# Self attention of an encoder-decoder layer: score groups side by side, eight PSUM banks in one round, value products summed in SBUF

## The chip, the cores and the metric

The kernel runs on one core of a Trainium2 chip. The metric is the device time of one execution in microseconds (us); the time before is the median of three runs, 2924.71 us (2924.21 to 2924.82). A core has five engines with a queue of instructions each: PE (matrix products into PSUM), DVE (vector), ACT (scalar), POOL (GpSimd) and SP, which here issues the DMAs. PSUM has eight banks of 128 x 512 float32; DVE and ACT read it, POOL doesn't. An engine runs its queue in order and waits on semaphores for the others.

## The reference

One encoder layer over a context of 77 rows and one decoder layer over 2048 rows, for two batch elements, all in float32; the width is 512, with 16 heads of 32. The part that the change touches is the decoder's causal self attention with a relative bias:

```python
def _mha(xq, xkv, w_in, b_in, w_out, b_out, bias):
    ...
    q = (xq @ wq.T + bq).reshape(Bq, Tq, H, hd).transpose(0, 2, 1, 3)
    k = (xkv @ wk.T + bk).reshape(Bq, Tk, H, hd).transpose(0, 2, 1, 3)
    v = (xkv @ wv.T + bv).reshape(Bq, Tk, H, hd).transpose(0, 2, 1, 3)
    scores = jnp.einsum('bhqd,bhkd->bhqk', q, k) / jnp.sqrt(jnp.asarray(hd, xq.dtype))
    scores = scores + bias[None]
    attn = jax.nn.softmax(scores, axis=-1)
    out = jnp.einsum('bhqk,bhkd->bhqd', attn, v)
    out = out.transpose(0, 2, 1, 3).reshape(Bq, Tq, D)
    return out @ w_out.T + b_out
...
causal = jnp.where(jnp.arange(Tt)[None, :] > jnp.arange(Tt)[:, None], -jnp.inf, 0.0)
sb = _rel_bias(dec_rel_self, Tt, Tt) + causal[None]
yn = _ln(y, dec_n1_s, dec_n1_b)
y = y + _mha(yn, yn, dec_sa_in_w, dec_sa_in_b, dec_sa_out_w, dec_sa_out_b, sb)
```

After it come cross attention to the encoder's 77 rows and a feed-forward layer.

## The kernel before

**Units, pieces and pairs.** Self attention runs first, up to about 1776 us of the span, and the feed-forward layer with the cross attention after it. It is cut into 128 *units* in the order b, m, g, t: batch element (2), block of 512 query rows (m, 4), group of four heads (g, 4), tile of 128 query rows in the block (t, 4). A unit has i + 1 blocks of 128 keys, with i = 4 m + t. `pieces(i)` cuts these into pieces of at most four blocks (4, 4, 4, 3 for fifteen; 4, 4, 3, 2 for thirteen), and the loop at the end takes two consecutive pieces of a unit as a *pair*. With m = 0 and 1 a unit has one pair, with m = 2 and 3 two; there are 192 pairs.

**What is done for a piece.** `scores` takes four banks, one per head, and writes one 128 x (up to 512) product into each (L361): a *score group*. The four heads stand in four quarters of PE's rows, so the four products run beside each other. DVE then empties bank after bank into `pp`, with the row maximum (L370); the last two blocks of a unit get bias and mask on the way (L377), and the unit's maximum is put together (L384). The exponentials are ACT's, one per head over the unit's whole row (L387). For m of 1 and over they are held back in `late_exps`, and `exps(k)` issues k of them at a chosen place.

**The turn.** `turn(pair)` transposes the probabilities on PE (L411), four 128 x 128 tiles into one bank: a *load*. For m of 1 and over a load holds the four heads of one key block, so a full pair has eight. Each load is copied to `pts`, by ACT (L417) or by DVE (L415); before, the first half of the loads is ACT's and the second half DVE's, and an exponential is issued after the fourth load and one at the end. A load needs the exponentials of all four heads.

**The values.** `values` multiplies the turned probabilities with `vv` (L428), 32 rows of output per head, and sums over all key blocks of the unit in bank 7, where the four tiles of a group of heads stand beside each other. At the group's end the bank is copied whole to `oT` (L434). A unit later `divide` multiplies it by the reciprocals of the sums (L447 on PE, L448 on DVE), and some units later `out_job` uses it.

**The banks.** `bank()` hands out banks in turn. Seven go round, and the eighth is the values'. A matmul that gets a bank waits until the engine that reads its last contents has done so, and PE's queue waits with it.

**The order.** Everything is issued in the order in which the loop calls it, each engine in its own queue. Scoring is two units ahead: a unit's pieces are scored when the unit two before has been turned as far (`may_score`). Between two units stands `slot(n + 1)`: the projections (`q_job`, `k_job`, `v_job`, `out_job`: four matmuls of 512 columns, one bank each), the norms of the next block, the encoder's stages (in the first 27 units) and a first cross attention (in units 65 to 92). So in the long rows the order on PE is: turn, scores, values, scores; turn, slot, scores, values, scores; and so on. The loop's body, before:

```python
            turn(pair)
            ...
            if ends and n + 1 < end:
                slot(n + 1)
            if may_score():
                score_next()
            exps(2 if units[n][1] == 1 else 1)
            for p in pair:
                values(*p)
            while may_score() and (len(pair) > 1 or units[n][1] == 0):
                score_next()
```

The numbers of units count from 0: unit 54 is b = 0, m = 3, g = 1, t = 2 and has fifteen key blocks.

Of the kernel before, what the change touches and what calls it, by code (L numbers as in the profile page):

```python
# [10 lines left out]
F32 = mybir.dt.float32  # L11
AF = mybir.ActivationFunctionType
ALU = mybir.AluOpType
# [4 lines left out]
P = 128  # L18
B, T, S, D = 2, 2048, 77, 512
H, HD, DFF = 16, 32, 2048  # L20
NC = D // P
NF = DFF // P
HC = P // HD
MB = 512
NMB = T // MB
TB = MB // P
# [28 lines left out]
def tile_encoder_decoder(ctx: ExitStack, tc: tile.TileContext, ins, out):  # L55
    nc = tc.nc
# [92 lines left out]
    with (  # L149
# [7 lines left out]
        vv = ac.tile([P, T // P, D], F32, name="vv")  # L157
# [6 lines left out]
        oT_all = ac.tile([P, 6, TB * P], F32, name="oT")  # L164
        bv = ac.tile([P, D], F32, name="row_sa_bv")
        bo = ac.tile([P, D], F32, name="row_dec_sa_out_b")
        psum = ps.tile([P, 8, 512], F32, name="psum")
        count = {"bank": 0, "banks": 7, "pts": 0, "oT": 0, "mm": 0}

        def bank():  # L170

            i = count["bank"] % count["banks"]
            count["bank"] += 1
            return psum[:, i, :]

        def in_turn(what, tile):
            i = count[what] % tile.shape[1]
            count[what] += 1
            return tile[:, i, :]

        def rows4(r):
            return slice(r * HD, (r + 1) * HD)


        nTs, qTs, ots, sums_of = {}, {}, {}, {}
# [132 lines left out]
        units = [(b, m, g, t) for b in range(B) for m in range(NMB) for g in range(NC) for t in range(TB)]  # L318
# [20 lines left out]
        def exps(k):  # L339

            for _ in range(min(k, len(late_exps))):
                late_exps.pop(0)[1]()
# [52 lines left out]
        got = {}  # L395

        def turn(pieces):

            first = units[pieces[0][0]][1] == 0
            loads = []  # L400
            for n, k0, kn in pieces:
                ks = range(k0, k0 + kn)
                if first:
                    loads += [[(n, k, r) for k in ks] for r in range(HC)]
                else:
                    loads += [[(n, k, r) for r in range(HC)] for k in ks]
            for o, load in enumerate(loads):
                pt = bank()
                pts = in_turn("pts", pts_all).rearrange("p (x q) -> p x q", q=P)
                for x, (n, k, r) in enumerate(load):  # L410
                    nc.tensor.transpose(pt[:, ts(x, P)], state[n]["p"][r][:, ts(k, P)], ident)  # L411
                    got[n, k, r] = pts[:, x, :]
                w = len(load) * P
                if o % 2 if first else o >= (len(loads) + 1) // 2:
                    nc.vector.tensor_copy(pts[:, : len(load), :], pt[:, :w])  # L415
                else:
                    nc.scalar.copy(pts[:, : len(load), :], pt[:, :w])  # L417
                if o == min(3, len(loads) - 1):
                    exps(1)
            exps(1)  # L420

        def values(n, k0, kn):
            b, m, g, t = units[n]
            i = m * TB + t
            for k in range(k0, k0 + kn):
                ot = psum[:, 7, :].rearrange("p (t q) -> p t q", q=P)
                for r in range(HC):
                    nc.tensor.matmul(  # L428
                        ot[rows4(r), t, :], vv[:, k, ts(g * HC + r, HD)], got.pop((n, k, r)),
                        start=(k == 0), stop=(k == i),  # L430
                    )
                if t == TB - 1 and k == i:
                    o = ots[b, m, g] = in_turn("oT", oT_all)
                    (nc.vector.tensor_copy if m else nc.scalar.copy)(o, psum[:, 7, :])  # L434

        def divide(b, m, g):

# [455 lines left out]
        for x, (b, m) in enumerate(blocks):  # L893
            u = x * NU
            first = m == 0
# [77 lines left out]
        def slot(n):  # L973
            for f in light[n]:
                f()
            for _, run, _ in jobs[n]:
                load_next()
                run(loaded[ran[0]])
                ran[0] += 1
            if n == 5:  # L980
                load_next()
# [35 lines left out]
        def w_1_load(i):  # L1017

            nc.sync.dma_start(w_1[:, :, ts(i, D)], wchunk("dec_ff1_wT", i * D))
# [220 lines left out]
        def may_score():  # L1240

            if at[0] == len(stream):
                return False
            n, k0, kn = stream[at[0]]
            same = n >= 2 and units[n][:2] == units[n - 2][:2]
            return n < 2 or turned_to[n - 2] >= (min(k0 + kn, size[n - 2]) if same else size[n - 2])

        def score_next():
            n, k0, kn = stream[at[0]]
            scores(n, k0, kn)  # L1250
            scored_to[n] = k0 + kn
            at[0] += 1
# [4 lines left out]
        i = 0  # L1257
        while i < len(stream):
            n = stream[i][0]
            pair = [p for p in stream[i : i + 2] if p[0] == n]  # L1260
            while scored_to.get(n) != size[n]:
                score_next()
            while any(u == n for u, _ in late_exps):
                exps(1)
            ends = pair[-1][1] + pair[-1][2] == size[n]
            if ends:
                for f in ahead[n + 1]:
                    f()
            turn(pair)
            if n == end - 2:  # L1270
                for _, k0, _ in pair:
                    w_1_load(k0 // 4)
            turned_to[n] = pair[-1][1] + pair[-1][2]
            if ends and n + 1 < end:
                slot(n + 1)
            if may_score():
                score_next()
            exps(2 if units[n][1] == 1 else 1)
            for p in pair:
                values(*p)  # L1280
            while may_score() and (len(pair) > 1 or units[n][1] == 0):
                score_next()
            i += len(pair)

        xt_ring += [sb.tile([P, D], F32, name="xt", tag="xt", bufs=2) for _ in range(2)]
# [71 lines left out]
```

## Time and profile before

| | |
|---|---|
| median of three runs | 2924.71 us |
| the profiled execution | 2926.65 us, of which its span 2924.9 us |
| granted PE clock, mean | 0.99 |
| self attention, m = 2 of b = 0 (407 to 640 us) | PE 231.9, DVE 196.7, ACT 135.7, POOL 7.1 us busy of 233 |
| self attention, m = 3 of b = 0 (640 to 929 us) | PE 285.4, DVE 246.9, ACT 177.9, POOL 7.2 us busy of 289 |
| score products, L361 | 353.2 us on PE |
| turns, L411 | 546.2 us on PE |
| value products, L428 | 278.9 us on PE |

How to read it: the page gives each engine's busy time, and PE's is modelled, since its matmuls overlap: a matmul that waits for its bank can count as busy. So the turns are better judged by the time from their first instruction to the first of what follows, and by the lines that name a releaser ("<-DVE mx L377": the wait before it was ended by DVE's instruction at line 377 on tile mx). In the order of time each line is a run of equal instructions: its start, its length, the engine, the line of the code, the operation, the tiles and their shapes, and how many; L361 and L428 show two instructions for a matmul.

### The profile page before, as it was taken

How to read it: one execution, taken by the hardware profiler on the slowest of the kernel's cores; microseconds unless marked ns; L12 is line 12 of the kernel's file. 1: busy time of each engine (PE TensorE's matmuls, PEld its weight loads, DVE VectorE, ACT ScalarE, POOL GpSimd, SP SyncE). 2: the span in 40 equal slices, each digit the busy share in tenths (PEclk: the TensorE clock that was granted, in tenths of full speed). 3: DMA queues.
4: the chain of work that ended last, by engine and by line, in shares of the span. 5: the costliest groups of instructions: out<-in, count | busy, mean ns of one | idle time of the engine just before them, and what ended most of it. 6: DMA issues, size and time to landing. Idle time of an engine off the chain costs nothing.

```text
span 2924.9 us, 60758 instructions
## 1 busy us (share of the span) xinstructions
PE 2867.7 (98%) x24440; PEld 2017.3 (69%) x24440; DVE 2121.4 (73%) x5958; ACT 1303.9 (45%) x2431; POOL 732.7 (25%) x594
## 2 busy tenths in 40 slices
PE   8899999999999999999999999999999999999999
PEld 5457666666666556666666667877777777777788
DVE  4767688888987788788888894757575757575745
ACT  3344456546665446555556673323232323232321
POOL 0100000000000101000000004565556364646464
PEclk9899999999999999999999999999999999999999
DMA  6413301201111502211201116000001000000000
GB/s 173 101 54 112 100 16 52 67 16 45 34 41 56 141 23 73 71 27 54 55 16 38 41 31 206 1 30 1 29 1 38 10 29 1 30 1 30 1 15 15
DMA packets 117644, 137.11 MB, mean 47 GB/s; under 512 B 18240, under 2 KB 73072, under 8 KB 117234
## 3 DMA queue, kind: packets, MB, share of 16 engines
q1 hardware_dynamic: 117362, 133.22, 15.7%
q8 instruction: 192, 3.15, 0.4%
q14 instruction: 90, 0.74, 0.1%
HBM read 111.33 MB, written 21.86 MB: 46 GB/s over the span
## 4 chain that ended last, share of the span: by engine, by line
PE 84%; DVE 13%; ACT 1%; issue 1%; DMA 1%; SPq 0%; POOL 0%; DVEq 0%; ACTq 0%; POOLq 0%
PE psum L1160 13%; PE psum L411 12%; PE psum L1131 11%; PE psum L361 10%; PE psum L428 7%; DVE pp L370 5%; PE psum L230 4%; PE psum L811 4%; PE psum L206 4%; PE psum L751 4%; PE psum L242 4%; PE psum L217 3%; DVE pp L377 3%; PE psum L791 2%; PE psum L765 1%
## 5 line engine op out<-in xcount | busy, mean ns | idle before, releaser
L387 ACT ACTIVATE pp<-pp,nm 128x128 f32<-128x128 f32 (+15 forms) x512 | 614.2, 1210 | 197.9 <-DVE nm L384 195.1
L370 DVE TENSOR_SCALAR_CACHE_REDUCE pp<-psum 128x512 f32<-128x512 f32 (+3 forms) x1024 | 558.0, 589 | 53.7 <-PE psum L361 51.7
L411 PE MATMUL psum<-ident,pp 128*128 128x128 f32 x4352 | 546.2, 278 | 17.7 <-DVE mx L377 11.8
L411 PEld LDWEIGHTS psum<-ident,pp 128*128 128x128 f32 x4352 | 472.7, 142 | 130.5 <-DVE pp L370 56.5
L417 ACT COPY pts<-psum 128x512 f32<-128x512 f32 (+3 forms) x592 | 298.8, 577 | 517.2 <-PE psum L411 391.4
L1114 POOL TENSOR_TENSOR vv<-pp 128x512 f32<-128x512 f32 x320 | 425.6, 1345 | 168.2 <-PE psum L1131 148.0
L361 PE MATMUL psum<-kT,q 32*128 32x512 f32 (+3 forms) x2560 | 353.2, 579 | 7.5 <-DVE mx L377 3.5
L415 DVE COPY pts<-psum 128x512 f32<-128x512 f32 (+2 forms) x544 | 329.8, 659 | 41.0 <-PE psum L411 39.3
L428 PEld LDWEIGHTS psum<-pts,vv 128*32 128x32 f32 x8704 | 226.2, 110 | 123.9 <-issue 116.9
L428 PE MATMUL psum<-pts,vv 128*32 128x128 f32 x8704 | 278.9, 276 | 0.0
L1146 DVE TENSOR_TENSOR kT<-kT,psum 128x512 f32<-128x512 f32 x256 | 166.7, 681 | 114.6 <-PE psum L1131 108.9
L276 POOL TENSOR_TENSOR rstd<-rstd,mhalf 128x1 f32<-128x1 f32 x32 | 18.2, 570 | 920.7 <-DVE rstd L275 860.7
L377 DVE CUSTOM_DVE_ANT_0 pp<-psum,bias 128x256 f32<-128x256 f32 (+1 forms) x512 | 209.6, 409 | 24.2 <-PE psum L361 16.7
L361 PEld LDWEIGHTS psum<-kT,q 32*128 32x128 f32 x2560 | 119.7, 184 | 152.2 <-issue 97.8
L1149 ACT ACTIVATE kT<-kT,vecs 128x256 f32<-128x256 f32 x256 | 115.1, 499 | 194.2 <-DVE kT L1146 194.2
L1160 PE MATMUL psum<-vv 128*128 128x256 f32 x768 | 176.9, 381 | 0.0
L1131 PE MATMUL psum<-oT,vv 128*128 128x256 f32 x736 | 166.5, 380 | 0.0
L1160 PEld LDWEIGHTS psum<-vv 128*128 128x128 f32 x768 | 143.1, 190 | 26.8 <-issue 9.5
L1144 ACT COPY kT<-psum 128x512 f32<-128x512 f32 x124 | 69.7, 589 | 205.9 <-DVE kT L1146 135.5
L1131 PEld LDWEIGHTS psum<-oT,vv 128*128 128x128 f32 x736 | 138.8, 190 | 24.5 <-issue 6.4
L1114 DVE TENSOR_TENSOR vv<-kT 128x512 f32<-128x512 f32 x160 | 136.3, 867 | 12.3 <-PE psum L1160 12.1
L257 POOL TENSOR_TENSOR xr<-xr,row_dec_sa_out_b 128x512 f32<-128x512 f32 x30 | 38.1, 1273 | 372.8 <-DMA xr<-in_x_dram 354.5
(175 smaller groups left out, 3961.9 us busy)
## 6 DMA issues: line engine op xcount, KB each, us to landing
wqk<-in_dec_sa_in_wT_dram SPq DMA_DIRECT2D x64, 256.0 KB, 3.8
bias<-tz SPq DMA_DIRECT2D x128, 128.0 KB, 3.7
wbig<-in_dec_sa_in_wT_dram SPq DMA_DIRECT2D x8, 1024.0 KB, 8.1
vv<-in_enc_ff_wT_dram SPq DMA_DIRECT2D x8, 1024.0 KB, 5.5
wbig<-in_dec_sa_out_wT_dram SPq DMA_DIRECT2D x8, 1024.0 KB, 7.6
vv<-y SPq DMA_DIRECT2D x32, 256.0 KB, 3.4
out_dram<-vv SPq DMA_DIRECT2D x32, 256.0 KB, 2.0
xt<-in_x_dram SPq DMA_DIRECT2D x30, 256.0 KB, 3.7
```

What stands on the lines that cost most here:

```text
L361: nc.tensor.matmul(banks[r][:, : kn * P], q[rows4(r), ts(t, P)], kT[rows4(r), g, k0 * P : (k0 + kn) * P], start=True, stop=True,)
L370: nc.vector.tensor_scalar(p[:, k0 * P : (k0 + far) * P], s[:, : far * P], 1.0, None, ALU.mult, ALU.max, accum_out=st["mx"][:, r, c : c + 1],)
L377: nc.vector.tensor_tensor_reduce(p[:, (i + 1) * P - w : (i + 1) * P], s[:, far * P : kn * P], biases[b, m, g][:, r, 2 * P - w :], 1.0, LOW ...
L387: nc.scalar.activation(p, p, AF.Exp, bias=nm, accum_out=to)
L411: nc.tensor.transpose(pt[:, ts(x, P)], state[n]["p"][r][:, ts(k, P)], ident)
L415: nc.vector.tensor_copy(pts[:, : len(load), :], pt[:, :w])
L417: nc.scalar.copy(pts[:, : len(load), :], pt[:, :w])
L428: nc.tensor.matmul(ot[rows4(r), t, :], vv[:, k, ts(g * HC + r, HD)], got.pop((n, k, r)), start=(k == 0), stop=(k == i),)
L1114: engine.tensor_tensor(dst, quarter(*parts[0], n), quarter(*parts[2], n), SIGN[parts[1]])
L1131: nc.tensor.matmul(mm[:, ts(f, TOK)], a[:, c, ts(f, P)], b[:, c, :], start=(c == 0), stop=(c == 1))
L1146: nc.vector.tensor_tensor(dst, dst, got, SIGN[sign])
L1160: nc.tensor.matmul(mm[:, t, :], lhs[:, c, ts(t, P)], rhs[:, c, :], start=(n == 0 and c == 0), stop=(n == 3 and c == 1),)
```

## The change

The loop now scores as far as it may before the values, and the values of a pair are one call. They get a bank of the round, which now has eight, and are summed there over the pair alone; ACT copies them out, to `oT` for a unit's first pair, and to a tile `more` for a later one, which GpSimd adds to `oT`. Of a turn's loads DVE gets the first three eighths and ACT the rest. The exponential in the middle of a turn is gone, and after the scores three are issued in place of two where m = 1.

```diff
-        count = {"bank": 0, "banks": 7, "pts": 0, "oT": 0, "mm": 0}
+        count = {"bank": 0, "banks": 8, "pts": 0, "oT": 0, "mm": 0}
...
-                if o % 2 if first else o >= (len(loads) + 1) // 2:
+                if o % 2 if first else o < 3 * len(loads) // 8:
                     nc.vector.tensor_copy(pts[:, : len(load), :], pt[:, :w])
                 else:
                     nc.scalar.copy(pts[:, : len(load), :], pt[:, :w])
-                if o == min(3, len(loads) - 1):
-                    exps(1)
             exps(1)
 
-        def values(n, k0, kn):
+        def values(pieces):
+
+            n = pieces[0][0]
             b, m, g, t = units[n]
-            i = m * TB + t
-            for k in range(k0, k0 + kn):
-                ot = psum[:, 7, :].rearrange("p (t q) -> p t q", q=P)
+            ks = [k for _, k0, kn in pieces for k in range(k0, k0 + kn)]
+            ot = bank()[:, :P]
+            for k in ks:
                 for r in range(HC):
                     nc.tensor.matmul(
-                        ot[rows4(r), t, :], vv[:, k, ts(g * HC + r, HD)], got.pop((n, k, r)),
-                        start=(k == 0), stop=(k == i),
+                        ot[rows4(r), :], vv[:, k, ts(g * HC + r, HD)], got.pop((n, k, r)),
+                        start=(k == ks[0]), stop=(k == ks[-1]),
                     )
-                if t == TB - 1 and k == i:
-                    o = ots[b, m, g] = in_turn("oT", oT_all)
-                    (nc.vector.tensor_copy if m else nc.scalar.copy)(o, psum[:, 7, :])
+            if t == 0 and ks[0] == 0:
+                ots[b, m, g] = in_turn("oT", oT_all)
+            dst = ots[b, m, g][:, ts(t, P)]
+            if ks[0] == 0:
+                nc.scalar.copy(dst, ot)
+            else:
+                more = sm.tile([P, P], F32, name="more", tag="more", bufs=1)
+                nc.scalar.copy(more, ot)
+                nc.gpsimd.tensor_tensor(dst, dst, more, ALU.add)
...
             if may_score():
                 score_next()
-            exps(2 if units[n][1] == 1 else 1)
-            for p in pair:
-                values(*p)
             while may_score() and (len(pair) > 1 or units[n][1] == 0):
                 score_next()
+            exps(3 if units[n][1] == 1 else 1)
+            values(pair)
             i += len(pair)
```

## The prediction

> **What bounds the kernel now.** I read the page's busy times first, then its chain, then the groups, then PE and DVE in order of time around one turn of the longest rows.
>
> ```profile
> PE 2867.7 (98%) x24440; PEld 2017.3 (69%) x24440; DVE 2121.4 (73%) x5958; ACT 1303.9 (45%) x2431; POOL 732.7 (25%) x594
> PE 84%; DVE 13%; ACT 1%; issue 1%; DMA 1%; SPq 0%; POOL 0%; DVEq 0%; ACTq 0%; POOLq 0%
> ```
>
> PE sets the end, but 13% of the chain (about 380 us) runs through DVE, by line L370 and L377: DVE emptying score banks. So PE waits for banks at times, although its row shows 98%. The groups say where:
>
> ```profile
> L411 PEld LDWEIGHTS psum<-ident,pp 128*128 128x128 f32 x4352 | 472.7, 142 | 130.5 <-DVE pp L370 56.5
> L417 ACT COPY pts<-psum 128x512 f32<-128x512 f32 (+3 forms) x592 | 298.8, 577 | 517.2 <-PE psum L411 391.4
> L415 DVE COPY pts<-psum 128x512 f32<-128x512 f32 (+2 forms) x544 | 329.8, 659 | 41.0 <-PE psum L411 39.3
> ```
>
> The turns (L411) wait for DVE; ACT idles between its copies, DVE hardly (41.0 us before 544 copies). Now unit 53 to 54 in order of time (start, length, what); PE:
>
> ```profile
> 754.99 1.14 PE L361 MATMUL psum<-kT,q 32*128 32x512 f32 x8
> 756.06 1.52 PE L428 MATMUL psum<-pts,vv 128*32 128x128 f32 x48
> 757.51 1.14 PE L361 MATMUL psum<-kT,q 32*128 32x512 f32 x8
> 758.58 2.46 PE L411 MATMUL psum<-ident,pp 128*128 128x128 f32 x20
> 761.25 0.66 PE L411 MATMUL psum<-ident,pp 128*128 128x128 f32 x4 [0.22 <-DVE mx L377]
> 762.13 1.09 PE L411 MATMUL psum<-ident,pp 128*128 128x128 f32 x8 [0.22 <-DVE mx L377]
> 763.15 1.14 PE L361 MATMUL psum<-kT,q 32*128 32x512 f32 x8
> 764.23 1.96 PE L428 MATMUL psum<-pts,vv 128*32 128x128 f32 x64
> 766.11 1.14 PE L361 MATMUL psum<-kT,q 32*128 32x512 f32 x8
> ```
>
> and DVE:
>
> ```profile
> 756.15 0.69 DVE L370 TENSOR_SCALAR_CACHE_REDUCE pp<-psum 128x512 f32<-128x512 f32 x1 [0.30 <-PE psum L361]
> ...
> 758.67 0.42 DVE L370 TENSOR_SCALAR_CACHE_REDUCE pp<-psum 128x256 f32<-128x256 f32 x1
> ...
> 762.11 0.16 DVE L384 TENSOR_REDUCE nm<-mx 128x1 f32<-128x5 f32 x1
> 762.19 2.48 DVE L415 COPY pts<-psum 128x512 f32<-128x512 f32 x4
> 764.59 0.68 DVE L370 TENSOR_SCALAR_CACHE_REDUCE pp<-psum 128x512 f32<-128x512 f32 x1
> ```
>
> Call the two score groups of a pair A and B, the values V, the eight loads of the turn l0 to l7. With A's start as 0: V 1.07, B 2.52, turn 3.59, next A 8.16. The same turn with no wait takes 3.64 (several in the trace), here 4.57: l5 and l6 wait for DVE. DVE empties A from 1.16 to 3.68 (0.61 a bank), B, a unit's last group with bias and maximum, to 7.28 (0.88 a bank), and only then copies its loads.
>
> **The change, part by part.** All durations from this execution; the sum goes against its 2926.65 us and then moves to the median 2924.71 (1.9 less).
>
> *Scores side by side.* In the trace a group that follows another one starts 0.96 after it, where V or a turn starts 1.07 after. In the built order 135 groups follow a group directly, 21 before: 114 x 0.11 = 12.5 us less on PE at most. It counts only where the turn that follows isn't DVE's.
>
> *What DVE must do before the turn.* B moves ahead of V, but DVE was not idle in between (0.07 from 3.61 to 3.68), so it finishes B at 7.21 in place of 7.28. PE: A 0, B 0.96, V 2.03, turn 3.48, l6 still waits for B's last bank: the turn ends at 8.1 again, not 7.1. Moving B hides nothing here.
>
> *The copies change hands.* Before, ACT copied the first half of a turn's loads, DVE the rest; now DVE the first three of eight, ACT the last five (L415 544 to 392, L417 592 to 744). DVE sheds 152 x 0.62 = 94 us and the 24 copies of oT (16.4 us); that is off the path unless DVE ends a wait. With eight banks round and eight loads, the next A takes the banks of l0 to l3 and B those of l4 to l7 where no slot lies between. Before (seven banks), A took l1 to l4, three of them ACT's, the fourth DVE's first. Now A's first three wait for all of DVE's copies, and those stand behind B's emptying in DVE's queue: 7.13 + 0.69, then 0.62 and 0.62: l2's bank is free at 9.05. So r=2 of the next A starts at 9.1 in place of 8.1, B at 10.06, V at 11.13, the next turn at 13.01. Before that turn started at 767.18, which is 12.19. **Cost +0.8 us**, and behind the waiting matmul all of PE is queued; what is late next is V and the second turn, whose slot then gives DVE time, so it doesn't add up.
>
> The same walk for the other turns that have no slot behind them, with the emptying times of their last group (0.74 a bank for three blocks, 0.53 for two, starts 1.16, 0.95 or 0.73 after a group of 512, 384 or 256):
> - four-block rows (m = 3), t = 1, last group three blocks: DVE done 6.67, l2 free 8.5, +0.90, 4 per batch element; t = 2 (the walk above) +0.84, 3; t = 0 (two blocks behind 512): wait 0.6, less 0.22 and earlier starts, +0.31, 3; t = 3 +0.05, 3; t = 2 of the last g, where V follows the turn, +0.4.
> - m = 2: t = 2 behind a last group of four alone: DVE done 4.75, turn ends 5.64, l2 free 6.6: +0.91, 3, and +0.4 once. t = 1, where three groups now run before V: before A, V, B, C took 5.97 (481.25 to 487.21); V hid 1.88 of DVE's work on A. Now C's banks are A's, so C waits for DVE's 3.06 on A, and V comes after: +0.86, 4. t = 0 and 3: 0. One turn that waits 1.7 (DVE late out of the slot; the slot starts later now, DVE doesn't) gives back 1.2.
> - m = 1: a slot behind every turn; 8 turns, -0.11 or 0: -0.9. Where blocks change: three groups before V +0.5 and +1.1; five groups before V, where V now hides emptying: -1.7.
> - m = 0: one group a unit, order as before: 0.
>
> Per batch element: 0.93 + 3.6 + 2.5 + 0.15 + 0.4 + 2.7 + 0.4 + 3.4 - 1.2 - 0.9 + 0.5 + 1.1 - 1.7 = 12. Two: **+24 us**. Each wait is good to about 0.3 us over some 50 places: +9 to +39.
>
> *V leaves its bank.* 192 copies on ACT, 128x128: the row of L417 in that shape has 268 ns: 51 us, plus 152 x 0.52 = 79 for loads, less 8 x 0.57: ACT +126 us. Cover: in long rows a unit has 10 copies, four exps of 2.0 and two V copies, 13.7 of some 18.6 us. Queued behind the V copy are the next turn's copies, first needed 1.8 us into that turn; l7 reuses V's bank 3.2 us into it. Without the cover, an exp (2.0) ahead of the V copy would hold the turn. The three exps that m = 1 now runs in a row (1.1 each) can end after the turn wants them when the slot keeps ACT busy: 0 to 1.4 us at 8 places, I take 0 since most turns there wait for DVE anyway; range 0 to +11.
>
> *GpSimd adds.* 64 of 128x128. Bounds: 0.55 (128x1, L276) and 1.27 (128x512, L257); by size 0.73: 47 us on an engine that is busy 7 us in the 233 us of m = 2 (407 to 640 us). The sum is read by L448 a unit later, some 15 us: 0. Does it slow DVE? L415's copy has 0.68 both inside and outside GpSimd's 1.27 us adds (13 inside): 0, with 0 to 0.55 x 64 = 35 as the far bound.
> The Trainium skill (GPSIMD Engine Reference, section Specifications) speaks against this part: GpSimd shares its SBUF interface with VectorE and contends with certain VectorE forms, those in a two-port mode or with two SBUF inputs. By that an add could hold DVE for its length, and 64 of them would add up to the 47 us just named; the copies from PSUM in this trace show none of it, so the row decides.
>
> *The eighth bank.* Where slots run several jobs (m = 0 and 1), one more bank may free PE earlier: 0 to -6, since the waits there that name DVE or ACT are few; I take 0.
>
> **Forecast:** 2926.65 + 24 - 1.9 = 2949 us, own range 2930 to 2970.
>
> **The rivals.**
> 1. *Faster: the waits in the turns go and none comes back.* It needs DVE to reach l3 to l6's banks in time, that is, B's emptying to move ahead with B. For it: the row of L411 has 56.5 us behind L370 alone. Against it: DVE has no gap to move into. If so, 30 turns x 0.85 and 12.5: 2887. It decides if DVE idles over 0.9 us between A and B in most pairs.
> 2. *No change:* A's wait is real but a third of what I have (DVE's copies run as soon as their load is there, ahead of the emptying's end). Against it: one queue, in order. 24 - 24 = about 2925.
> 3. *Much slower: ACT.* If the V copy stands behind an exp that waits for DVE's maximum, the turn's copies and the next groups wait 1 us or more in the 64 long pairs: 2949 + 64 = 3013. Against it: the exps ahead of V are of a unit scored a pair earlier, so their maximum is long there.
>
> **How the numbers follow.** Forecast 0.62, rival 1 0.15, rival 2 0.10, rival 3 0.13. Below 0.2% (5.8 us) a measurement can't tell a change here. Faster takes rival 1 and a small share of the rest, 0.17; same 0.11; slower 0.72. The range runs from 2912 to 2980: the forecast's own, all of no change, and the near parts of the rivals.
>
> **What would show it.** In the new trace, behind unit 54's turn, the third matmul of the score group starts about 1 us after the second, released by DVE's copy (L415); turns behind a last group of three or four blocks still take 4.4 to 4.6; V follows B after 1.07; ACT stands idle before most copies of L417; PE's idle time that names ACT stays under 10 us. It is wrong if the score groups behind turns take 0.96 (rival 1 or 2), or if turns wait for ACT (rival 3).

## The result, and the profile after

The changed kernel takes 2973.89 us (median of five runs, 2971.24 to 2975.92) against 2924.71: 1.0165 times as long, 95% interval 1.0153 to 1.0176, or 49 us more. Its profiled execution has a span of 2969.5 us against 2924.9, so 44.6 us of the difference can be looked for in the traces. All of it lies in self attention, whose last value product on PE starts at 1818.3 us in place of 1774.2.

The page after: busy times and the groups of turn and copies (busy, mean ns | idle before, by releaser).

```profile
PE 2881.6 (97%) x24440; PEld 2061.6 (69%) x24440; DVE 2013.0 (68%) x5782; ACT 1421.8 (48%) x2767; POOL 763.4 (26%) x658
...
L411 PE MATMUL psum<-ident,pp 128*128 128x128 f32 x4352 | 544.5, 278 | 44.1 <-ACT pp L387 32.3 <-DVE mx L377 9.9 <-DVE nT L301 0.5
L411 PEld LDWEIGHTS psum<-ident,pp 128*128 128x128 f32 x4352 | 475.9, 142 | 106.5 <-ACT pp L387 39.3 <-issue 29.1 <-DVE mx L377 28.0
L417 ACT COPY pts<-psum 128x512 f32<-128x512 f32 (+2 forms) x744 | 379.4, 586 | 196.9 <-PE psum L411 157.1 <-issue 17.7 <-DVE pp L370 14.7
```

DVE lost 108 us of work and ACT took 118, and yet PE is later. The 56.5 us that the turns waited for DVE's emptying (L370) no longer head the list; a wait that was small before does: PE waits 32.3 us for exponentials (ACT, L387), 2.4 before. The rest of the new time is hidden in PE's "busy" and shows only in the order of time. Unit 54 on PE:

```profile
771.02 2.56 PE L411 MATMUL psum<-ident,pp 128*128 128x128 f32 x20
773.80 0.66 PE L411 MATMUL psum<-ident,pp 128*128 128x128 f32 x4 [0.22 <-DVE mx L377]
774.68 1.09 PE L411 MATMUL psum<-ident,pp 128*128 128x128 f32 x8 [0.22 <-DVE mx L377]
775.70 2.95 PE L361 MATMUL psum<-kT,q 32*128 32x512 f32 x16
778.58 1.95 PE L428 MATMUL psum<-pts,vv 128*32 128x128 f32 x64
```

and on DVE:

```profile
774.65 0.16 DVE L384 TENSOR_REDUCE nm<-mx 128x1 f32<-128x5 f32 x1
774.73 1.88 DVE L415 COPY pts<-psum 128x512 f32<-128x512 f32 x3
...
776.86 0.69 DVE L370 TENSOR_SCALAR_CACHE_REDUCE pp<-psum 128x512 f32<-128x512 f32 x1 [0.25 <-PE psum L361]
```

The turn waits for DVE twice, as before (4.68 us from its first instruction to A, before 4.57). Two score groups without a wait take 2.1 us (see the kernel with DVE one load earlier, below); here they take 2.95, because DVE copies l0 to l2 only when it has emptied B (774.73), and is done at 776.6. The wait shows in PE's weight loads (PEld), which precede the matmuls:

```profile
775.70 0.66 PEld L361 LDWEIGHTS psum<-kT,q 32*128 32x128 f32 x4 [0.17 <-issue]
776.66 0.73 PEld L361 LDWEIGHTS psum<-kT,q 32*128 32x128 f32 x10 [0.31 <-DVE pts L415]
```

A's third matmul starts at 776.66, released by DVE's copy. That is 9.05 after the score group A ahead of the turn (767.61), where the walk of the prediction has it; its second matmul waits too, so the third comes 0.60 after the second, not about 1. Start to start A takes 1.50, B 1.38, V 1.88.

Turn start to turn start, pair by pair, the two traces differ like this (us, both batch elements):

| place | forecast | measured |
|---|---|---|
| m = 3, t = 1 and t = 2, first pairs | +13.0 | +11.3 |
| m = 3, t = 0 (but the first) and t = 3 (but the last), first pairs | +2.2 | -0.2 |
| m = 2, t = 1: three groups ahead of V | +6.9 | +6.8 |
| m = 2, t = 2 | +6.3 | +7.5 |
| m = 2, t = 0 | -2.4 | -2.9 |
| m = 2 to 3, unit 47 and 111 | +2.2 | +2.2 |
| m = 2 to 3, unit 48 and 112: five groups ahead of V | -3.4 | +5.9 |
| m = 1 (the step to m = 2 in it) | -0.8 | +7.3 |
| m = 3 to 0, unit 63 and 127 | 0 | +8.3 |
| rest | 0 | -1 |

So the sum has two halves. The places where DVE's copies or a third group make PE wait came as worked out. Some 21 us more (5.9, 7.3 and 8.3) stand where the forecast had nothing, or a gain. In m = 2, t = 2 the size is nearly right, but the cause is another; unit 34, PE and then ACT:

```profile
438.39 0.65 PE L428 MATMUL psum<-pts,vv 128*32 128x128 f32 x16
438.96 0.55 PE L411 MATMUL psum<-ident,pp 128*128 128x128 f32 x3
440.93 3.39 PE L411 MATMUL psum<-ident,pp 128*128 128x128 f32 x29 [1.42 <-ACT pp L387]
```

```profile
439.15 0.27 ACT L439 COPY more<-psum 128x128 f32<-128x128 f32 x1 [1.62 <-PE psum L428]
439.31 1.47 ACT L387 ACTIVATE pp<-pp,nm 128x1408 f32<-128x1408 f32 x1
```

The fourth head's exponential stands behind the copy of V in ACT's queue. ACT idles 1.62 us until V is done on PE; the exponential ends at 440.8, and the turn that needs it waits until then (5.28 us, before 3.99). The loop allows this: an exponential that the few `exps` calls left over is issued just ahead of the turn that needs it, and by then V's copy is queued.

### The profile page after: what moved, and what is told of

It reads as the page before. It is cut to its first block, busy times and chain, and to the rows that moved or that the text cites. A ratio compares the mean times of both kernels' runs of the same rounds, so it can differ in the third digit from the quotient of the medians.

```text
span 2969.5 us, 61184 instructions
## 1 busy us (share of the span) xinstructions
PE 2881.6 (97%) x24440; PEld 2061.6 (69%) x24440; DVE 2013.0 (68%) x5782; ACT 1421.8 (48%) x2767; POOL 763.4 (26%) x658
## 5 line engine op out<-in xcount | busy, mean ns | idle before, releaser
L387 ACT ACTIVATE pp<-pp,nm 128x128 f32<-128x128 f32 (+15 forms) x512 | 615.6, 1214 | 162.8 <-DVE nm L384 160.1
L370 DVE TENSOR_SCALAR_CACHE_REDUCE pp<-psum 128x512 f32<-128x512 f32 (+3 forms) x1024 | 554.4, 590 | 115.4 <-PE psum L361 113.6
L411 PE MATMUL psum<-ident,pp 128*128 128x128 f32 x4352 | 544.5, 278 | 44.1 <-ACT pp L387 32.3
L417 ACT COPY pts<-psum 128x512 f32<-128x512 f32 (+2 forms) x744 | 379.4, 586 | 196.9 <-PE psum L411 157.1
L440 POOL TENSOR_TENSOR oT<-oT,more 128x128 f32<-128x128 f32 x64 | 29.2, 457 | 1003.6 <-ACT more L439 1003.6
L361 PEld LDWEIGHTS psum<-kT,q 32*128 32x128 f32 x2560 | 158.9, 184 | 177.2 <-issue 92.9
L415 DVE COPY pts<-psum 128x512 f32<-128x512 f32 (+2 forms) x392 | 237.2, 649 | 36.8 <-PE psum L411 36.5
L377 DVE CUSTOM_DVE_ANT_0 pp<-psum,bias 128x256 f32<-128x256 f32 (+1 forms) x512 | 209.5, 409 | 23.0 <-PE psum L361 15.7
```

The costliest lines, as they stand in the source:

```text
L361: nc.tensor.matmul(banks[r][:, : kn * P], q[rows4(r), ts(t, P)], kT[rows4(r), g, k0 * P : (k0 + kn) * P], start=True, stop=True,)
L370: nc.vector.tensor_scalar(p[:, k0 * P : (k0 + far) * P], s[:, : far * P], 1.0, None, ALU.mult, ALU.max, accum_out=st["mx"][:, r, c : c + 1],)
L377: nc.vector.tensor_tensor_reduce(p[:, (i + 1) * P - w : (i + 1) * P], s[:, far * P : kn * P], biases[b, m, g][:, r, 2 * P - w :], 1.0, LOW ...
L387: nc.scalar.activation(p, p, AF.Exp, bias=nm, accum_out=to)
```

## Experiments: one part undone at a time

Every run is compared with the kernel before on the same chip (2925 to 2926 us there). The differences below are to the kernel after, 2973.89. Most of these kernels ran only two or three times, and the kernel after spreads over 4.7 us in its five runs, so a difference in the total of less than some 5 us says little; sums by place are from one profiled execution each.

**The copies' split undone** (ACT the first half of the loads, DVE the second).

```diff
-                if o % 2 if first else o < 3 * len(loads) // 8:
+                if o % 2 if first else o >= (len(loads) + 1) // 2:
```

> The changed kernel with the old split of a turn's copies alone (first half ACT, second half DVE). Bank theory (next A waits for DVE's copies of l0 to l2): in unit 54 the next A no longer waits (group to group 0.96), but B now waits for DVE's copy of l7, about 0.65 in place of 0.85, so about -0.2 to -0.4 on some 25 turns and about 5 us less in all, 2963 to 2972. Exponential theory (the turns wait for exponentials that ACT runs too late): ACT sheds 152 copies but the exponentials stay where they are, so the long turns of 5.28 (m = 2, t = 2), 5.5 (first turn of m = 3) and 7.8 to 8.4 (last unit of a batch element) stay; 2968 to 2974.

2973.81 us (ratio 1.0168, 1.0139 to 1.0198): no change, at the far end of what was expected. Fourteen of the sixteen first pairs of m = 3, t = 1 and t = 2 gave back 0.25 or more, and many of t = 0, t = 3 and m = 2 took 0.24 to 0.38 each: A no longer waits (0.96 in unit 54, 1.50 after), but B does (1.66, 1.38 after), since now all of B's banks (l4 to l7) hang on DVE. This execution also lost 5.1 us more than that of the kernel after to a lower PE clock, which is explained below. Four copies on DVE are one too many for B; it isn't only A that can wait.

**The exponentials' places undone.**

```diff
                     nc.scalar.copy(pts[:, : len(load), :], pt[:, :w])
+                if o == min(3, len(loads) - 1):
+                    exps(1)
             exps(1)
...
-            exps(3 if units[n][1] == 1 else 1)
+            exps(2 if units[n][1] == 1 else 1)
```

> The changed kernel with the old places of the exponentials alone (one after a turn's fourth load, one at its end, 2 or 1 after the scores). Bank theory alone: unit 54's waits stay as they are and the total falls by less than 8 us. Exponential theory: the waits of L411 that name ACT's exponentials (71.6 us in 53 places in the changed kernel) go, the turns of 5.28 become 4.0, the last units' 7.8 to 8.4 become about 4; 20 to 30 us less, 2943 to 2953. Since DVE then ends some of those waits, I expect 2950.

3010.06 us (1.0292, 1.0262 to 1.0322): 36 more where some 24 less was expected. ACT in unit 54's turn:

```profile
782.27 0.59 ACT L417 COPY pts<-psum 128x512 f32<-128x512 f32 x1
782.75 2.01 ACT L387 ACTIVATE pp<-pp,nm 128x2048 f32<-128x2048 f32 x1
...
784.74 2.04 ACT L417 COPY pts<-psum 128x512 f32<-128x512 f32 x4
```

The exponential in the middle, which cost nothing while the second half of the loads was DVE's, now stands ahead of ACT's own copies of l4 to l7; B takes 2.51 in place of 1.38, and nearly every first pair of m = 3 loses 1.2 to 2.0 (unit 49 and 113 nothing). At the same time unit 63 and 127 gave back 4.15 and 4.79 and unit 48 and 112 1.24 and 2.09. So the missing exponential does cost something there, but its old place goes with the old split only.

**The order undone** (A, V, B, with the eight banks).

```diff
             if may_score():
                 score_next()
-            while may_score() and (len(pair) > 1 or units[n][1] == 0):
-                score_next()
             exps(3 if units[n][1] == 1 else 1)
             values(pair)
+            while may_score() and (len(pair) > 1 or units[n][1] == 0):
+                score_next()
```

> The changed kernel with the old order alone: A, V, B (eight banks, new copies, V in its own bank). Bank theory: the next A still waits for DVE's copies of l0 to l2 (0.9 behind last groups of three or four blocks), the 12.5 us of groups side by side are lost in part, the turns of m = 2, t = 1 (three groups before V) win 0.84 back each, 8 of them, and five groups before V win some 3 us back at each of 2 places; 2960 to 2970. If putting the groups side by side were itself the loss, it would fall to 2945 or less.

2972.9 us (1.0165, 1.0135 to 1.0194): no change, where some 4 to 14 less was expected. m = 2, t = 1 gives back 1.88 eight times, 15 us, more than it had lost; but with DVE's copies first the wait stays in A (unit 54: turn 4.33, A 2.25, V 1.88, B 1.07: 9.53 against 9.44), and t = 0 and t = 3 of m = 3 lose 0.6 to 1.0 each at most places. Unit 49 and 113 lose 4.0 and 2.6 more, so the sum hides gains and losses of 10 us and over.

**The eighth bank undone** (seven go round, V in the eighth).

```diff
-        count = {"bank": 0, "banks": 8, "pts": 0, "oT": 0, "mm": 0}
+        count = {"bank": 0, "banks": 7, "pts": 0, "oT": 0, "mm": 0}
...
-            ot = bank()[:, :P]
+            ot = psum[:, 7, :P]
```

> The changed kernel with seven banks in the round and V always in the eighth, the rest as changed. Bank theory: B's fourth bank is then A's first, so every B that follows A directly waits for DVE to empty it, about 0.9 us at 114 places, less where V's copy was waited for: 3040 to 3080. If the eighth bank bought nothing, it stays at 2974.

3052.61 us (1.0437, 1.0407 to 1.0468): 79 more, 15 of them by a lower PE clock. With two groups side by side the eighth bank is not an extra, it is what the order stands on.

## Experiments: one cause removed at a time, and together

**DVE copies the last three loads.**

```diff
-                if o % 2 if first else o < 3 * len(loads) // 8:
+                if o % 2 if first else o >= len(loads) - 3 * len(loads) // 8:
```

> The kernel after, but DVE copies the last three loads of a turn (l5 to l7) in place of the first three; how many each engine copies stays. Theory (the score group behind a turn waits for DVE's copies, because its banks were those of l0 to l2 and DVE comes to them last): A's banks are then all copied by ACT, which idles; B's banks l5 to l7 are free from about 7.2 + 0.6 + 0.6 + 0.7 = 9.1 after A, about when B starts. From turn to turn m = 3 t = 1 and t = 2 get back 0.75 to 0.85 each (14 places in the long pairs' first turns), 12 in all: about 2962. Rival (the groups wait for DVE wherever its copies stand, since DVE empties banks until then): B waits by what A waited, no change, 2970 to 2976. The turns of m = 2 t = 2 (5.28 long) stay as long, by both.

2964.43 us (1.0132, 1.0103 to 1.0162), near the theory's 2962. Unit 54, PE:

```profile
776.51 1.09 PE L411 MATMUL psum<-ident,pp 128*128 128x128 f32 x8 [0.22 <-DVE mx L377]
777.53 2.13 PE L361 MATMUL psum<-kT,q 32*128 32x512 f32 x16
```

The same copies by the same engine at the same time, but on banks that are wanted a group later: A and B take 2.13 in place of 2.95. Fourteen of the sixteen first pairs of m = 3, t = 1 and t = 2 gave back 0.70 to 0.82; the other two (unit 49 and its like in the other batch element, unit 113, whose turn of 5.59 waits for an exponential) took 0.22 more. This shows the cause at these places: the banks, not the amount of copying.

**The next unit's exponentials ahead of V's copy.**

```diff
             exps(3 if units[n][1] == 1 else 1)
+            while ends and any(u == n + 1 for u, _ in late_exps):
+                exps(1)
             values(pair)
```

> The kernel after, but where a unit ends, all exponentials still held back for the next unit are issued ahead of the values' copy on ACT, in place of being forced behind it when the turn comes. Theory (the turns of 5.28 in m = 2 t = 2, and those of 7.8 and 8.4 at the two changes of m from 3 to 0, wait for an exponential that stands behind the values' copy in ACT's queue, and that copy waits for the values on PE): these turns fall to about 4.0, but the score groups behind them then wait for DVE's copies of about 0.9, so 6 places give 0.4 to 1.3 each, and the two changes 4 each: 10 in all, about 2963. Rival (the exponential waits for DVE's maximum, late itself): the values' copy is then queued behind the wait, turns stay as long, 2972 to 2980.

2966.84 us (1.0141, 1.0111 to 1.017), near the theory's 2963, but in part by luck. The turn of unit 42 (m = 2, t = 2) falls from 5.29 to 4.00, and then A takes 1.40 and B 1.26, as the theory said: DVE's copies are next. The eight first pairs of m = 2, t = 2 give 4.2 in all, and 4.5 come from unit 48, 49, 112 and 113, which the theory didn't name. Unit 63 and 127 are a miss: -1.5 and +1.4, where 4 each was expected. In neither does the exponential stand behind V's copy, in the kernel after already; unit 63 there, ACT:

```profile
928.72 0.40 ACT L387 ACTIVATE pp<-pp,nm 128x128 f32<-128x128 f32 x1 [1.06 <-DVE nm L384]
...
930.31 1.99 ACT L387 ACTIVATE pp<-pp,nm 128x2048 f32<-128x2048 f32 x1
...
932.29 0.24 ACT L439 COPY more<-psum 128x128 f32<-128x128 f32 x1
```

The four short exponentials of the next unit, with m = 0, are issued as soon as it is scored, ahead of the long one that is still owed, and they wait 1.06 for DVE's maximum; V's copy comes last. Behind unit 127 no unit follows: ACT simply has two of its long exponentials to do when its turn begins. The edit moves nothing here: PE's waits are the same with it and without (2.43 in unit 63; 1.20 and 1.65 in unit 127). What differs is the clock behind the wait: the last 29 matmuls of the turn take 4.88 after and 3.39 here in unit 63, 4.88 and 6.25 in unit 127.

**At most two groups ahead of V.**

```diff
-            while may_score() and (len(pair) > 1 or units[n][1] == 0):
+            if may_score() and (len(pair) > 1 or units[n][1] == 0):
                 score_next()
             exps(3 if units[n][1] == 1 else 1)
             values(pair)
+            while may_score() and (len(pair) > 1 or units[n][1] == 0):
+                score_next()
```

> The kernel after, but at most two score groups are issued ahead of the values; a third and more follow behind them. Only places change where three or more groups ran ahead: m = 2 t = 1 (8 pairs), the steps from m = 2 to m = 3 (five groups, 2), m = 1 to 2 and a few more. Theory (C waits for DVE's emptying of A, and the values that would hide it stand behind C): m = 2 t = 1 gives back 1.9 to 2.0 each (16), the steps 2 each and 1 each at four more places: 24 in all, about 2949. Rival (the wait only moves into the turn behind, which DVE bounds): about half, 2960 to 2966.

2968.28 us (1.0145, 1.0116 to 1.0175): 5.6 less where 24 was expected. m = 2, t = 1 gave back 1.09 eight times, not 1.9: C still waits behind V (1.79). Of the steps to m = 3, unit 47 and 111 gave 1.41 each, unit 48 and 112 next to nothing, and unit 49 and 113 took 3.1 and 3.4 more. In unit 48 V now comes behind two groups, and the five take 7.3 in place of 10.1; but the turns of unit 48 and 49 grow from 5.50 and 5.59 to 8.83 and 8.69. Unit 49's turn, PE:

```profile
669.85 0.44 PE L411 MATMUL psum<-ident,pp 128*128 128x128 f32 x2
...
672.13 0.33 PE L411 MATMUL psum<-ident,pp 128*128 128x128 f32 x1 [1.84 <-ACT pp L387]
673.90 4.71 PE L411 MATMUL psum<-ident,pp 128*128 128x128 f32 x29 [1.44 <-ACT pp L387]
```

PE waits for two exponentials, since two are left over behind V's copy now, and the 29 matmuls behind them take 4.71, where the same number takes 3.39 in the fence of unit 34: the granted clock of that stretch (674 to 678) is 0.67. The group that completes a unit's scores is now issued behind the `exps` call of its pair, which finds nothing to issue.

**All three.** The three edits above in one kernel.

> The kernel after with all three edits of this call: DVE copies the last three loads, exponentials of the next unit are issued ahead of the values' copy at a unit's end, at most two score groups ahead of the values. If the three causes are separate, the gains add: 12 + 10 + 24 = 46 less than after, about 2928, and a little less if the turns of m = 2 t = 2 give back all, 2920 to 2930. Rival (they share one bound, DVE's time): the sum falls short by half, about 2950.

2920.05 us (eight runs; ratio 0.9978, 0.9967 to 0.9989). Alone the three gave 9.5, 7.1 and 5.6, together 54: the expected 46 and more. They are not separate. Part of the surplus was settled by leaving the third out:

> Two of the three edits: DVE copies the last three loads, and the next unit's exponentials go ahead of the values' copy; all groups ahead of the values as in the kernel after. The three together gave 54 less than after, alone they gave 9.5, 7.1 and 5.6. Theory (a turn of m = 2 t = 2 waits for the exponential or, with that gone, the groups behind it for DVE's copies, the same time by two ways, so only both edits free it): these 6 places give 1.28 each here too, as with all three, in place of 0.5 and 0; with 9.5 + 7.1 that is some 21 to 26 less than after: 2948 to 2953. Rival (the surplus comes from the third edit, which takes away the long stalls of PE after which its clock is granted at half): the sum of the two alone, 2955 to 2958.

2947.94 us (1.0076, 1.0053 to 1.0099), 26 less than after. The first pairs of m = 2, t = 2 give 0.9 to 1.29 each, all eight, where the exponentials' edit alone gave 0.28 to 0.77 and the copies' edit nothing: one wait stood behind the other. Unit 49 and its like now give 1.13, for the same reason. And with all three the turns of unit 48 and 49 take 4.90 and 4.41, not 8.83 and 8.69: the third edit pays only where the exponentials are early.

The other part is the PE clock. Summed up to 1840 us, the time that a granted clock below 1 takes away is 22.2 us before, 27.3 after, 35.8 with the copies' edit, 30.7 with each of the other two, 35.8 with the first two, 20.5 with all three. The loss comes in stretches of 3.41 us, or a multiple of it, at half clock: 1.71 us lost for each 3.41. So the spans of after and of the copies' edit are 4.9 us apart, but 13.4 without the clock, the theory's 12; and with all three 6.8 of the 50.5 between the spans are clock. The Trainium skill (TensorE: Matmul & The Clock Gate, section What's actually happening) says that half the clock is granted after a window of 3.4 us in which PE was idle, and that the windows run free of the program. The traces agree: from 40 to 1840 us all eight half-clock stretches of the kernel after begin on one grid of 3.413 us, to within 0.002 us, and so do those of every other kernel here, each trace with a grid of its own. And the grid tells which stall is paid twice. C's stall of m = 2, t = 1 lasts about 3.28 us at eight places in each of six kernels (after, the first two edits alone and together, and the old split and the old exponentials). Of these 48, 15 begin within 0.40 us of the grid, so that the stall nearly fills one step of it; 14 of them are followed by half clock (V then takes 3.1 to 3.6 in place of 1.88), and none of the other 33. Whether such a stall is paid twice is thus chance of the one execution, and so is part of the differences above.

**DVE one load earlier** (l4 to l6), with all three.

```diff
-                if o % 2 if first else o >= len(loads) - 3 * len(loads) // 8:
+                if o % 2 if first else 0 < len(loads) - o - 1 <= 3 * len(loads) // 8:
```

> All three edits, but DVE copies l4 to l6 of eight in place of l5 to l7 (in general as many, ending one load earlier). Theory (with l7 on DVE, B behind a turn of m = 3 t = 0 or t = 3 or of m = 2 t = 3 starts 0.2 late, because l7's copy takes 0.69 on DVE against 0.5 on ACT and ends last): these about 20 places give 0.2 each, 4 in all, about 2916, and the turns of t = 1 and t = 2 stay, since l4 to l6 are all B's banks. Rival (ACT's copy of l7 stands behind its copies or an exponential): no change or 1 to 3 more, 2920 to 2923.

2915.62 us (six runs; ratio 0.9969, 0.9955 to 0.9982), the theory's 2916, and the lowest median of all kernels here: 9 us below the kernel before. Seventeen of the first pairs of m = 3, t = 0 and t = 3 and of m = 2, t = 3 give 0.30 to 0.37 each. PE in unit 54 is at its best:

```profile
753.25 1.09 PE L411 MATMUL psum<-ident,pp 128*128 128x128 f32 x8 [0.22 <-DVE mx L377]
754.28 2.10 PE L361 MATMUL psum<-kT,q 32*128 32x512 f32 x16
756.31 1.95 PE L428 MATMUL psum<-pts,vv 128*32 128x128 f32 x64
```

From start to start A 0.96, B 1.07, V 1.88; only the turn still waits (4.68), for B's emptying. The traces of this kernel and of before differ by 11.8 us in self attention. That this is close to the 12.5 of the groups side by side shows little: 6.8 are lost at unit 63 and 127, 18.6 gained over many other places, and with the third edit only 119 groups follow another one, not 135.

**Never more than two groups in a pair**, with all three edits.

```diff
             values(pair)
-            while may_score() and (len(pair) > 1 or units[n][1] == 0):
+            while may_score() and units[n][1] == 0:
                 score_next()
```

> All three edits, but for m of 1 and over never more than two score groups in a pair: a third is left to the next pair, which scores behind its slot, in place of being issued behind the values. Theory (C, behind the values, still waits for DVE's emptying of A: 1.69 to 1.8 in place of 0.96 in m = 2 t = 1, and 0.8 to 1.5 each in the three groups behind the values at the step to m = 3): 8 times 0.8 and twice 3: 12 less, about 2908. Rival (the groups come a pair later, so a unit's exponentials come later and turns wait for them): as with all three or slower, 2920 to 2940.

3225.14 us (1.1026, 1.0994 to 1.1058): the rival, and far more than it asked. In m = 2 the wait of C does go (t = 1: 1.4 to 1.9 less than with all three, eight times). But pairs with two groups each never make up the one that was put off, so in m = 3 a unit's last group is scored just ahead of its turn. The page's group, and three windows around unit 54's turn (length, then PE, PEld, DVE, ACT and POOL busy, then the clock):

```profile
L411 PE MATMUL psum<-ident,pp 128*128 128x128 f32 x4352 | 635.2, 302 | 250.3 <-ACT pp L387 241.6 <-DVE mx L377 7.6 <-DVE nT L301 0.5
```

```profile
808.00:812.00 4.00, 0.95 (x2) 0.36 (x2) 1.11 (x8) 4.00 (x5) 0.00 (x0) 0.51 0.00 0
812.00:816.00 4.00, 1.81 (x7) 1.52 (x8) 0.00 (x0) 3.35 (x6) 0.46 (x1) 0.50 0.01 4
816.00:819.00 3.00, 3.00 (x19) 3.00 (x19) 0.02 (x1) 2.16 (x4) 0.00 (x0) 0.61 0.00 0
```

PE waits for four exponentials in a row, and then begins the turn at half clock. Half clock stands for 239 us up to 1840 us in this kernel; counted only where PE's row is busy, that costs 76 us (18 with all three edits). So the stall is paid twice.

**DVE adds the later products from their bank**, in the best kernel.

```diff
-                more = sm.tile([P, P], F32, name="more", tag="more", bufs=1)
-                nc.scalar.copy(more, ot)
-                nc.gpsimd.tensor_tensor(dst, dst, more, ALU.add)
+                nc.vector.tensor_tensor(dst, dst, ot, ALU.add)
```

> All three edits with DVE on l4 to l6 (2915.6), but a unit's later value products are added by DVE straight from their bank, in place of ACT's copy to more (0.27) and GpSimd's addition (0.46), 64 times. Theory (GpSimd's additions cost DVE nothing, and DVE is late in the long rows): the addition, about 0.3 by the 0.69 of the addition of 512 columns out of a bank (L454), stands behind B's emptying and ahead of DVE's copies, and l7 waits for it since it reuses the values' bank; B behind a turn of m = 3 t = 1 and t = 2, and in part of t = 0 and t = 3, starts 0.2 to 0.3 later: 14 to 30 times, 4 to 9 more, 2919 to 2925. Rival (GpSimd's additions hold DVE up, for as long as they take): 64 times 0.46 comes back less what DVE's own addition takes, 2895 to 2910.

2917.34 us (ten runs, 2913.05 to 2919.71; best kernel 2914.29 to 2918.62): not to be told from the best kernel. By place the theory's low end is there: fourteen first pairs of m = 3, t = 1 and t = 2 take 0.18 to 0.20 more each, and six of m = 2, t = 2 0.1, 3.3 in all; t = 0 and t = 3 take nothing. The rival is out: without GpSimd's additions DVE's emptying (L370) has a mean of 590 ns, as with them and as before the change (589).

## Why the prediction was right

The forecast (2949, range to 2980) had the direction and the main cause; 25 us of the 49 were missing. The measured time lies above the forecast's own 2930 to 2970 and is inside the wider range only by the part that was added for the rivals, and what filled the gap is not what they describe: that much is luck.

- **The copies change hands: right in mechanism and size.** Unit 54 was put at +0.84 a pair, and from turn to turn it measured +0.84 (8.60 to 9.44). Moving DVE's copies to other loads took just this away. The small addition for t = 0 and t = 3 (2.2 us) wasn't there.
- **The turn still waits for DVE: right** (4.68; 4.4 to 4.6 before).
- **Three groups ahead of V: right**, 0.86 forecast, 0.84 measured. The experiment that undid it gave more than it had cost when V went between A and B, and 1.09 when C went behind V.
- **Five groups ahead of V: wrong sign**, -3.4 forecast, +5.9 measured. The step let V hide emptying, but V comes after all five groups now, and the turn behind it has nothing to hide (2.62 before, 2.61 after in unit 112). In unit 48 the last three groups take 2.44, 2.37 and 3.40, and PE reaches V with the clock at half (3.57 in place of 1.88). Over both units the groups add 2.1, V 3.4, and the first turns 2.2 (5.50 in place of 4.42, waiting for an exponential behind V's copy); the second pairs give 1.8 back, most of it because unit 48's turn was at half clock before.
- **The exponential taken out of the turn, at nothing: the step that failed.** The prediction asked whether the exponentials issued ahead of V's copy would hold it up (rival 3) and found them early enough; where the long pairs lost, that was so. It did not ask what is issued behind the copy, and its sum has no term for the exponential that the turn loses. With the exponential in the middle of the turn gone, one is left over where units are short on slots. In m = 2, t = 2, unit 48 and unit 49 it queues behind a copy that waits for PE. In unit 63 and 127 (8.3 us forecast as 0) it stands ahead of V's copy and is late all the same, in unit 63 behind four short exponentials; some 3 us of the 8.3 are half clock behind these waits. That the place of the exponential is the cause there too is shown by the kernel with the old places: both turns fall to 3.64.
- **m = 2, t = 2: the size by luck.** +6.3 was forecast for DVE's copies and +7.5 measured, but what makes these turns wait is the exponential; the copies come in only when that is gone.
- **m = 1: mis-sized**, -0.8 forecast, +7.3 measured. All three edits take part in bringing it back (two groups 4.5, the copies 1.8, exponentials 1.6 of 9.8); the cause by place stays open.
- **The eighth bank: mis-sized as a part by itself.** "0 to -6" held it against the old order; under the new one its absence costs 79.
- **GpSimd's additions: right, no cost that these runs can tell**; they take 0.46 each, not 0.73, and the contention that the prediction weighed against them does not show in DVE's emptying.
- **Groups side by side: right for each group** (0.96 against 1.07, unit 54 of the best kernel); the sum of 12.5 is a bound that no run here isolates.
- **A reading.** The prediction puts the 13% of the chain that run through DVE down to L370 and L377; its page gives these two lines 5% and 3%.
- **Rivals.** Rival 1 fails: DVE had no gap between A and B, and even in the best kernel the turn of unit 54 takes 4.68. Rival 2's price doesn't follow from its condition, since a third of the wait would leave about +8; the wait came in full. Rival 3 named the right engine and, but for unit 63, where its chain does stand (V's copy behind exponentials that wait for DVE's maximum), the wrong side of the copy. Of the signs, V follows B after 1.38, not 1.07, and "PE's idle time that names ACT stays under 10 us" failed by its own numbers (32.3) and pointed at the failed step.

Open: what unit 63 and 127 would take if the exponential still owed went earlier wasn't tried; the best kernel still loses 6.8 us there against before.

## What to carry to other kernels

When work moves between engines, ask of each copy which bank it frees and who takes that bank next: the late engine should hold the banks wanted last. When a wait for PE is put into another engine's queue, list what is issued behind it until the next thing that PE needs, not only what stands ahead of it. And undo parts in combination: here each repair alone brought 6 to 9 us, in part because the next wait stood right behind it, and all three together 54. When two kernels differ by a few us, compare their lost clock before the rest.

## What the runs showed of the hardware

A stall of PE can cost more than its length: half clock comes in stretches of 3.41 us or a multiple, 1.71 us for each 3.41, so 22 us of the kernel before and 27 of the one after are clock alone. The stretches begin on a grid of 3.413 us that is fixed within a trace and differs between traces. The same stall of 3.28 us was followed by half clock in 14 of the 15 cases in which it began within 0.40 us of the grid, and in none of 33 others. The window needn't be idle throughout: ahead of the half clock in unit 63 of the kernel after, PE's row is busy for 1.3 of the 3.41 us. A score group of 512 columns takes 0.96 when another group follows it and 1.07 when something else does.
